# Rotary attention: how a chunk's row maxima are turned and laid into the query rows

## The chip, the cores and the metric

One Trainium2 chip; the kernel runs on one of its cores. The metric is device time in microseconds (us) of one execution, the median of several runs. Engines are named as the profile names them: PE is TensorE (PEld its weight loads), DVE is VectorE, ACT is ScalarE, POOL is GpSimd, and SP is SyncE, which does nothing here but issue DMAs. Each engine works through its own queue in order and waits on semaphores for the others.

## The reference

The program is a chain of four two-part layers on an input of shape (4, 1024, 128). The change touches one part, the rotary attention of the second layer, with H = 16 heads of 8 channels:

```python
def _L1_attn_ref(x, w_qkv, w_out, b_out):
    qkv = x @ w_qkv
    q, k, v = jnp.split(qkv, 3, axis=-1)
    ...
    q = q * cos + rotate_half(q) * sin
    k = k * cos + rotate_half(k) * sin
    dots = jnp.einsum('bhid,bhjd->bhij', q, k) * scale
    attn = jax.nn.softmax(dots, axis=-1)
    out = jnp.einsum('bhij,bhjd->bhid', attn, v)
    ...
    return out @ w_out + b_out
...
x = x + _L1_attn_ref(_layernorm(x, axis=-1), ...)
```

Each query row's softmax needs the greatest score of that row first, so that the exponentials do not overflow.

## The kernel before

**Tiles.** A batch has 1024 queries and 16 heads. The attention takes four heads at a time: 4 batches x 4 groups of heads = 16 tasks, each with its rows in a ring of three sets of tiles. Of a head g, tile `qz` holds 64 partitions: rows 0 to 31 are the rotated queries, split into a rounded and a remaining part, with one column for each query; rows 32 and 33 are for the row maximum, rounded part and remainder; the other rows are zero. `kz` holds the keys in the same way with 1.0 in rows 32 to 63. A product of `kz` and `qz` over those 64 rows therefore gives the score minus the maximum (the stored maxima are negated), once rows 32 and 33 are filled.

**Two passes.** A task is cut into 2 chunks of 512 queries, a chunk into 8 units. There are 16 x 2 = 32 chunks and 256 units, and the main loop takes one unit in each step k. The *first pass* (`greatest`, L1165) multiplies 128 queries by 512 keys for two heads into a PSUM tile `two` of 128x1024, and one DVE instruction reduces it to the negated maxima of each row (`nm`, L1173). The *second pass* (`scores`, L1194, then `values`) runs 11 units later (`LEAD`): it multiplies 128 keys by the chunk's 512 queries into a PSUM tile `s`, ACT takes the exponential (`e`, L1201), and PE multiplies that by the values into `o`. A step has two halves, and each half issues on PE, in this order: an `s` product, two `two` products, an `s` product, eight `o` products. The first half takes heads 2 and 3 in the second pass, the second half heads 0 and 1.

**Between the passes: `shifted` (L1175).** It runs once for each chunk. At the end of the chunk's last first-pass step (k = 8c+7) DVE takes the smaller of the two halves' values (`least`, L1178), rounds it into one element of `top` (L1179) and puts the remainder beside it (L1180). `top` is a zeroed tile of 128 x 4 (128 queries each) x 4 heads x 32. One step later (k = 8c+8) PE transposes its four 128x128 pieces into a PSUM tile `tp` (L1184), which takes one of the two buffers of `two`. ACT copies the 128x512 result to `sh` (L1188), in which head g has its two rows at partitions 32g and 32g+1, and SP issues one DMA for each head (L1191), 2 rows of 512 floats, into rows 32 and 33 of `qz`. The second pass of the chunk starts at step k = 8c+11.

**Order of the work.** On PE the order is the program's own (a manual schedule of PE alone). On DVE, ACT, POOL and SP a planner orders the instructions by its estimates. `tile`s with several buffers are waited for by buffer. DMAs on SP take eight semaphores in turn. On SP's queue the other work of this stage is `l1_spread` (L1124): eight DMAs a task that bring the next task's queries and keys, with a POOL instruction that zeroes rows 32 and 33 (L1132). `l1_rings` (L1056) allocates the rings and has POOL fill them, among them two `top` tiles (L1068).

Of the kernel before, what the change touches and what calls it, by code (L numbers as in the profile page):

```python
# [11 lines left out]
F32 = mybir.dt.float32  # L12
F32R = mybir.dt.float32r
# [3 lines left out]
ALU = mybir.AluOpType  # L17
AX = mybir.AxisListType

P = 128  # L20
B, S, D = 4, 1024, 128
# [3 lines left out]
HALF = 512  # L25
# [7 lines left out]
RING = 3  # L33
# [516 lines left out]
class Macaron:  # L550
# [505 lines left out]
    def l1_rings(self, pool):  # L1056

        fill = self.nc.gpsimd
        for tag, n, shape, dtype in (
            ("qz", 2 * RING, [P, S], F32R), ("kz", 2 * RING, [P, S], F32R), ("top", 2, [P, 4, 4, 32], F32),
        ):
            self.ring[tag] = [self.t(pool, shape, f"{tag}{i}", dtype) for i in range(n)]
        for z in self.ring["top"]:
            fill.memset(z, 0.0)  # L1068
        for tag, value in (("qz", 0.0), ("kz", 1.0)):
            for z in self.ring[tag]:  # L1070
                for j in range(2):
                    fill.memset(z[64 * j + 32 : 64 * j + 64, :].bitcast(F32), value)
# [61 lines left out]
    def l1_attn(self, m, c1, f):  # L1134

        nc = self.nc
        scale = HD ** -0.5
        LEAD = 11
        v = nc.vector
        PE = mybir.EngineType.PE  # L1140
        with ExitStack() as ctx:
# [5 lines left out]
            wp = enter(self.sb("l1a"))  # L1147
# [4 lines left out]
            two = lambda shape=(P, S): self.t(p1, list(shape), "two")  # L1152
            qz, kz, tops = (self.ring[tag] for tag in ("qz", "kz", "top"))
            of = lambda z, n, g: z[2 * (n % RING) + g // 2][64 * (g % 2) : 64 * (g % 2) + 64, :]
# [10 lines left out]
            def greatest(unit, pair, nm):  # L1165
                n, (c, it, h) = unit // 16, (unit // 8, unit % 8 // 2, unit % 2)
                at = (c % 2 * 4 + it) * P
                s = two((P, 2, HALF))
                for j in (1, 0):
                    g = 2 * pair + j  # L1170
                    self.mm(s[:, j, :], of(qz, n, g)[:, at : at + P], of(kz, n, g)[:, h * HALF : (h + 1) * HALF])
                    yield
                v.tensor_reduce(nm[:, it, h, 2 * pair : 2 * pair + 2], s, AX.X, ALU.max, negate=True)  # L1173

            def shifted(chunk, nm):  # L1175
                top, n = tops[chunk % 2], chunk // 2
                least = self.t(wp, [P, 4, 4], "least")
                v.tensor_tensor(least, nm[:, :, 0, :], nm[:, :, 1, :], ALU.min)  # L1178
                v.tensor_copy(top[:, :, :, 0].bitcast(F32R), least)  # L1179
                v.tensor_tensor(top[:, :, :, 1], least, top[:, :, :, 0], ALU.subtract)  # L1180
                yield
                tp = two((P, HALF))
                for i in range(4):
                    nc.tensor.transpose(  # L1184
                        tp[:, i * P : (i + 1) * P], top[:, i].rearrange("p g r -> p (g r)"), self.c0["ident"]
                    )
                sh = self.t(wp, [P, HALF], "sh", F32R)
                nc.scalar.copy(sh, tp)  # L1188
                for g in range(4):
                    z = of(qz, n, g)[32:34, chunk % 2 * HALF : (chunk % 2 + 1) * HALF]  # L1190
                    nc.sync.dma_start(out=z.bitcast(F32), in_=sh[32 * g : 32 * g + 2, :].bitcast(F32))  # L1191
                yield

            def scores(unit, pair, es):  # L1194
# [137 lines left out]
            for k in range(units + LEAD + 1):  # L1332
                at = k
                first = k if k < units else None
                second = k - LEAD if 0 <= k - LEAD < units else None
                if k % 16 == 2 and RING <= k // 16 + 1 < 4 * B:
                    self.l1_spread(k // 16 + 1)
                    values_of(k // 16 + 1)
                if k == 1:
                    running.append(chain(*late))  # L1340
                if first is not None and first % 8 == 0:
                    nms[first // 8] = self.t(wp, [P, 4, 2, 4], "nm", bufs=3)
                es = {}
                for pair in range(2):
                    top = greatest(first, pair, nms[first // 8]) if first is not None else iter(())
                    part = scores(second, 1 - pair, es) if second is not None else iter(())
                    for one in (part, top, top, part, top):
                        next(one, None)
                    if pending:
                        unit, then = pending  # L1350
                        if unit % 8 == 0 and pair == 0:
                            o = self.t(pa, [P, HALF], "o")
                        values(unit, o, then, pair)
                if pending and unit % 8 == 7:
                    running.append(normalized(unit // 8, o))
                pending = (second, es) if second is not None else None
                if first is not None and first % 8 == 7:
                    running.append(shifted(first // 8, nms[first // 8]))
                running = [r for r in running if next(r, self) is not self]
# [543 lines left out]
```

## Time and profile before

| what | us |
|---|---|
| median of three runs | 2524.29 |
| lowest, highest | 2516.03, 2534.74 |
| the profiled execution | 2518.22 |
| its span | 2516.5 |
| the rotary attention in it | about 731 to 1545 |

| engine | busy in the span | share |
|---|---|---|
| PE | 2205.0 | 88% |
| DVE | 1746.7 | 69% |
| ACT | 1557.2 | 62% |
| POOL | 1073.8 | 43% |

The profile is one execution. A row of a group of instructions gives the line of the kernel, the engine, the operation, the tile written and the tiles read, the shapes and the count; then the busy time and the mean ns of one; then the idle time of that engine just ahead of them and what ended it. The timeline lists instructions by start, with equal neighbours merged: start, length, engine, line. Ends of matmuls are modelled and overlap, so the wall time of PE is read from starts. "issue" is idle time that no shown wait explains. Semaphores that DMAs raise are in the trace's records with their times.

### The profile page before, as it was taken

What the parts mean: (1) busy time and instruction counts of PE and PEld (TensorE: products, weight loads), DVE (VectorE), ACT (ScalarE), POOL (GpSimd) and SP (SyncE); (2) the same over time, 40 slices, a digit from 0 to 9 for tenths busy, and PEclk for the clock granted to TensorE, in tenths of its full rate; (3) what the DMA queues carried; (4) which work ended last, traced back from release to release, by engine and by line L of the source; (5) the groups of instructions that cost most, each with busy time, mean ns of one, the idle gap of its engine ahead of it and who ended that gap; (6) DMA issues with size and microseconds to landing.
All of it is one profiled execution on the core that took longest, in us unless ns stands there. A gap on an engine that the chain in (4) does not pass through costs nothing. (4 is left out here: it accounts for less than half of the span.)

```text
span 2516.5 us, 44437 instructions
## 1 busy us (share of the span) xinstructions
PE 2205.0 (88%) x15631; PEld 1402.3 (56%) x15631; DVE 1746.7 (69%) x2883; ACT 1557.2 (62%) x3917; POOL 1073.8 (43%) x1124
## 2 busy tenths in 40 slices
PE   4888784987979999999999999988998978688996
PEld 4877773767654334334333334577886978433332
DVE  2497999971448888888998992552656552398995
ACT  3766673844537777788787786554554554556564
POOL 3778874668352201220220000067554557254553
PEclk8999997988988999999999999999998989899998
DMA  6866763557651200210120000178665679100000
GB/s 229 289 202 228 245 203 128 166 159 228 188 178 56 56 19 18 65 56 18 52 83 20 25 2 11 32 251 286 214 204 194 211 256 300 57 1 5 9 5 17
DMA packets 135694, 312.40 MB, mean 124 GB/s; under 512 B 20752, under 2 KB 70032, under 8 KB 135344
## 3 DMA queue, kind: packets, MB, share of 16 engines
q1 hardware_dynamic: 110320, 253.28, 30.9%
q0 software_dynamic: 25152, 56.28, 7.9%
q8 instruction: 125, 2.05, 0.3%
q14 instruction: 97, 0.79, 0.1%
HBM read 259.86 MB, written 49.09 MB: 123 GB/s over the span
## 5 line engine op out<-in xcount | busy, mean ns | idle before, releaser
L1173 DVE TENSOR_REDUCE nm<-two 128x2 f32<-128x1024 f32 x512 | 623.1, 1223 | 72.0 <-PE s L593 43.7
L1201 ACT ACTIVATE e<-s 128x512 f32<-128x512 f32 x1024 | 558.4, 598 | 133.5 <-PE s L593 120.3
L296 POOL DMA_INDIRECT e_xg<-rows,g_source x333 | 359.0, 1078 | 483.9 <-DVE g_target L296 232.4
L296 ACT ACTIVATE e_h<-bank,e_w 128x128 f32<-128x128 f32 x1332 | 381.8, 378 | 252.6 <-PE bank L296 133.4
L870 POOL DMA_INDIRECT res<-e_y,g_target x333 | 380.4, 1142 | 177.7 <-issue 40.5
L296 PE MATMUL bank<-e_x,e_w 128*128 128x128 f32 x2664 | 385.1, 286 | 28.7 <-DMA e_w<-in_l0m_dram 17.8
L296 PE MATMUL bank<-e_w,e_h 128*128 128x128 f32 x2664 | 389.3, 283 | 10.9 <-ACT e_h L296 10.2
L593 PE MATMUL s<-qz,kz 64*128 64x512 f32 x1024 | 383.9, 450 | 2.9 <-ACT e L1201 2.8
L296 PEld LDWEIGHTS bank<-e_x,e_w 128*128 128x128 f32 x2664 | 350.1, 201 | 46.6 <-issue 22.6
L593 PE MATMUL two<-kz,qz 64*128 64x512 f32 x1024 | 359.3, 458 | 8.6 <-DVE nm L1173 8.0
L296 PEld LDWEIGHTS bank<-e_w,e_h 128*128 128x128 f32 x2664 | 352.3, 198 | 21.3 <-ACT e_h L296 15.5
L593 PE MATMUL o<-e,va 128*32 128x256 f32 x4096 | 329.2, 392 | 7.4 <-ACT os L1218 6.9
L593 PEld LDWEIGHTS s<-qz,kz 64*128 64x128 f32 x1024 | 157.5, 186 | 206.0 <-issue 97.4
L296 DVE TENSOR_TENSOR e_y<-bank,e_w 128x128 f32<-128x128 f32 x202 | 57.6, 286 | 212.9 <-PE bank L296 202.8
L593 PEld LDWEIGHTS o<-e,va 128*32 128x32 f32 x4096 | 81.6, 108 | 192.5 <-issue 174.2
L296 PE MATMUL bank<-c,e_xg 128*128 128x128 f32 x333 | 95.4, 291 | 102.9 <-DMA e_xg<-rows,g_source 72.1
L1132 POOL MEMSET qz<- 2x1024 f32 x52 | 49.1, 945 | 309.1 <-PE s L593 306.9
L296 ACT ACT_TABLE_LOAD x130 | 166.8, 1283 | 9.3 <-PE bank L296 7.0
L593 PEld LDWEIGHTS two<-kz,qz 64*128 64x128 f32 x1024 | 142.7, 188 | 26.7 <-DVE nm L1173 23.1
L296 ACT COPY e_x<-bank 128x128 f32<-128x128 f32 x181 | 49.7, 276 | 116.3 <-PE bank L296 112.6
L296 PEld LDWEIGHTS bank<-c,e_xg 128*128 128x128 f32 x333 | 48.9, 148 | 117.9 <-DMA e_xg<-rows,g_source 53.1
L1111 POOL TENSOR_TENSOR h<-h 128x512 f32<-128x512 f32 x12 | 15.4, 1281 | 227.0 <-DVE h L1107 172.5
(316 smaller groups left out, 3440.0 us busy)
## 6 DMA issues: line engine op xcount, KB each, us to landing
e_w<-in_l0m_dram SPq DMA_DIRECT2D x177, 578.0 KB
e_w<-in_l2m_dram SPq DMA_DIRECT2D x156, 578.0 KB
c_y<-res SPq DMA_DIRECT2D x30, 512.0 KB
stack<-s POOLq DMA_DIRECT2D x48, 256.0 KB
rows<-g_xt SPq DMA_DIRECT2D x16, 512.0 KB
qz<-stack SPq DMA_DIRECT2D x64, 128.0 KB
kz<-stack SPq DMA_DIRECT2D x64, 128.0 KB
e_xg<-rows,g_source POOLq DMA_INDIRECT x333
```

What stands on the lines that cost most here:

```text
L296: return call(*a, **k)
L593: self.nc.tensor.matmul(out, lhsT, rhs, start=start, stop=stop)
L870: ins = real.gpsimd.indirect_dma_start(out=res[:, :], out_offset=at(target[:, k : k + 1]), in_=y, in_offset=None)
L1111: nc.gpsimd.tensor_tensor(whole, turned[:, 0, :], turned[:, 1, :], ALU.add)
L1132: self.nc.gpsimd.memset(z[at + 32 : at + 34, :].bitcast(F32), 0.0)
L1173: v.tensor_reduce(nm[:, it, h, 2 * pair : 2 * pair + 2], s, AX.X, ALU.max, negate=True)
L1201: nc.scalar.activation(e, o, AF.Exp, scale=scale)
```

## The change

The two parts of the maxima of four heads and four blocks of queries are 32 columns. They are now kept side by side in a `top` of 128 x 4 heads x 2 parts x 4 blocks, without zeros between them. One transpose turns them into 32 rows of 128, ACT copies those to `sh` (now 32x128), and eight DMAs, one for each head and part, each take 4 rows of 128 floats and write them side by side as one row of 512 floats of `qz`. The two fills of `top` are gone. The three DVE instructions stay, with the block index innermost.

```diff
-            ("qz", 2 * RING, [P, S], F32R), ("kz", 2 * RING, [P, S], F32R), ("top", 2, [P, 4, 4, 32], F32),
+            ("qz", 2 * RING, [P, S], F32R), ("kz", 2 * RING, [P, S], F32R), ("top", 2, [P, 4, 2, 4], F32),
         ):
             self.ring[tag] = [self.t(pool, shape, f"{tag}{i}", dtype) for i in range(n)]
-        for z in self.ring["top"]:
-            fill.memset(z, 0.0)
...
                 least = self.t(wp, [P, 4, 4], "least")
-                v.tensor_tensor(least, nm[:, :, 0, :], nm[:, :, 1, :], ALU.min)
-                v.tensor_copy(top[:, :, :, 0].bitcast(F32R), least)
-                v.tensor_tensor(top[:, :, :, 1], least, top[:, :, :, 0], ALU.subtract)
+                halves = [nm[:, :, h, :].rearrange("p i g -> p g i") for h in range(2)]
+                v.tensor_tensor(least, *halves, ALU.min)
+                v.tensor_copy(top[:, :, 0, :].bitcast(F32R), least)
+                v.tensor_tensor(top[:, :, 1, :], least, top[:, :, 0, :], ALU.subtract)
                 yield
-                tp = two((P, HALF))
-                for i in range(4):
-                    nc.tensor.transpose(
-                        tp[:, i * P : (i + 1) * P], top[:, i].rearrange("p g r -> p (g r)"), self.c0["ident"]
-                    )
-                sh = self.t(wp, [P, HALF], "sh", F32R)
+                tp = two((32, P))
+                nc.tensor.transpose(tp, top.rearrange("p g r i -> p (g r i)"), self.c0["ident"])
+                sh = self.t(wp, [32, P], "sh", F32R)
                 nc.scalar.copy(sh, tp)
                 for g in range(4):
-                    z = of(qz, n, g)[32:34, chunk % 2 * HALF : (chunk % 2 + 1) * HALF]
-                    nc.sync.dma_start(out=z.bitcast(F32), in_=sh[32 * g : 32 * g + 2, :].bitcast(F32))
+                    for r in range(2):
+                        z = of(qz, n, g)[32 + r : 33 + r, chunk % 2 * HALF : (chunk % 2 + 1) * HALF]
+                        rows = sh[8 * g + 4 * r : 8 * g + 4 * r + 4, :]
+                        nc.sync.dma_start(out=z.rearrange("r (i q) -> r i q", i=4).bitcast(F32), in_=rows.bitcast(F32))
                 yield
```

## The prediction

> **What bounds the kernel now.** The page first: all that the change touches lies in the rotary attention, so I asked for the busy times of that stage and of one of its last chunks, where nothing else runs.
>
> ```profile
> core 0: us, PE busy (x) PEld busy (x) DVE busy (x) ACT busy (x) POOL busy (x), PEclk, DMA share, GB/s
> 731.00:1545.00 814.00, 790.02 (x6694) 319.47 (x6690) 690.86 (x769) 619.86 (x1146) 122.22 (x159) 0.98 0.13 37
> 1493.00:1515.00 22.00, 21.64 (x200) 8.53 (x198) 20.22 (x23) 18.31 (x35) 0.00 (x0) 1.00 0.01 2
> ```
>
> PE is busy 97% of the stage, DVE 85%, ACT 76%, at a granted clock of 0.98. PE's own order repeats every 1.23 us (the starts of `s` below: 1497.59, 1498.82, 1500.05), and the reduction of L1173 takes 1.223 us, so a late PE is not made up for, and neither is a late DVE.
>
> Then the groups of the touched lines and of the reduction in that stage:
>
> ```profile
> L1173 DVE TENSOR_REDUCE nm<-two 128x2 f32<-128x1024 f32 x512 | 623.1, 1223 | 72.0 <-PE s L593 43.7 <-PE two L593 24.4
> L1184 PE MATMUL two<-c,top 128*128 128x128 f32 x128 | 20.6, 285 | 4.1 <-DVE top L1180 3.6
> L1188 ACT CAST sh<-two 128x512 fp32r<-128x512 f32 x32 | 18.8, 586 | 27.3 <-PE two L1184 27.2
> ```
>
> The transposes and the copy are some 39 us of busy time, but of two engines and with overlaps. How much is on the path, the timeline of chunk 30 shows:
>
> ```profile
> 1493.76 0.19 DVE L1180 TENSOR_TENSOR top<-least,top 128x16 f32<-128x16 f32 x1
> 1493.86 1.22 DVE L1173 TENSOR_REDUCE nm<-two 128x2 f32<-128x1024 f32 x1
> ...
> 1494.10 0.63 PE L1184 MATMUL two<-c,top 128*128 128x128 f32 x4
> ...
> 1494.76 0.59 ACT L1188 CAST sh<-two 128x512 fp32r<-128x512 f32 x1 [0.32 <-PE two L1184]
> 1495.13 0.19 PEld L593 LDWEIGHTS two<-kz,qz 64*128 64x128 f32 x2 [0.30 <-DVE nm L1173]
> ...
> 1495.41 2.49 SPq L1191 DMA_DIRECT2D qz<-sh  x4
> ...
> 1500.05 0.49 PE L593 MATMUL s<-qz,kz 64*128 64x512 f32 x1
> ...
> 1500.39 0.39 PE L593 MATMUL s<-qz,kz 64*128 64x512 f32 x1
> ```
>
> Three things are to be seen. `tp` holds one of the two buffers of `two`, so the next `two` product waits for the reduction that runs beside the transposes (1493.86 + 1.22 = 1495.08; PE goes on at 1495.13): PE idles 0.30 us whatever the transposes take. The four issues hold SP for 2.49 us. And the chunk's second pass starts at 1500.05 with head 2, head 3 follows at 1500.39: these need the third and fourth DMA. By the trace's semaphore records a DMA of L1191 has landed 1.67 us (median of 128) after its issue began; the fourth began at 1497.33 and landed at 1499.0, so head 3 has 1.4 us to spare.
>
> Last the rows of single DMAs, for a price of the new ones:
>
> ```profile
> L1191 SPq DMA_DIRECT2D qz<-sh x128: 562/563/732, 756.9 to 1518.9; - x128
> L1130 SPq DMA_DIRECT2D qz<-stack x64: 302/371/1716, 626.0 to 1410.5; - x64
> L296 SPq DMA_DIRECT2D stack<-s x16: 518/539/750, 524.1 to 618.5; - x16
> L296 SPq DMA_DIRECT2D out_dram<-x x8: 332/332/350, 2295.1 to 2509.2; - x8
> ```
>
> (min/median/max ns that one issue holds SP.)
>
> **The change part by part.**
>
> *Three transposes fewer.* Four take 0.63 us from the first start, one alone 0.301: 0.11 us each, 0.33 a chunk. By the starts in the trace, in 17 of the 32 chunks PE then waits for the reduction as above (it resumes 0.05 us after it): nothing is gained. In the other 15 PE comes late to the transposes, with work of other parts in front of it, and 0.26 to 1.6 us pass after the reduction: there 0.33 is gained. Sum: 15 x 0.33 = 5.0 us. Bounds: 0, and 32 x 0.33 = 10.6. The new transpose has 32 weight columns where the old had 128; no row shows an f32 transpose of 32 columns, but a plain f32 product of 128 columns (`e_x`, `e_w`) has a median of 275 ns beside 273 for L1184, so it stays at one such step. [...]
>
> *A smaller copy.* 512 columns take 0.586; ACT copies of 128x128 from PSUM (`e_x<-bank`) have a median of 0.266. I take 0.28: 0.31 less a chunk. ACT is 76% busy, and after the copy PE waits for the reduction, not for `tp`'s buffer, which the copy frees at 1495.35 and the next but one `two` product needs at 1496.36. So it only brings the DMAs forward. The DVE instructions keep their 16 elements (175, 177, 189 ns). The two fills of `top` (0.52 us each on POOL, at 537 and 547, before this stage) have no waiter that the trace shows: 0, at most 1 us.
>
> *Four DMAs more a chunk, on SP's queue.* The starts of L1191's issues lie 0.641 us apart (mean; 0.563 and the semaphore step between). The new DMA is of the same kind, from `sh` to `qz` on the same queue, four pieces of 512 B in place of two of 2 KB; its price no row shows. From below: the cheapest issue on SP, 0.302, so 0.38 apart. From above: a DMA from SBUF whose pieces differ on both sides (`stack<-s`, 0.539) takes 0.207 more than one whose rows agree (`out_dram<-x`, 0.332); put on top of 0.563 that is 0.77, so 0.85 apart. I take 0.641, its nearest row, and the same 1.67 to land. The last issue then begins 7 x 0.641 = 4.49 after the first instead of 3 x 0.641 = 1.92: 2.56 later, less 0.33 and 0.31 from the two parts above: the last row lands 1.92 us later against the transposes. SP has idle time for it: behind the eight in its queue are only `l1_spread`'s loads, needed more than ten steps later.
>
> [...]
>
> *What is late next.* `s` of head 3 waits for DMAs seven and eight; queued behind it on PE are the eight `o` products and the next `two`, so DVE and ACT run dry with it and the stall is paid in full. Head 3's margin over its landing, from the trace: in ten of the 17 chunks 1.36 to 1.50, mean 1.43, so 0.49 each, 4.9; chunk 7 has 1.12: 0.8; the other six have 2.16 or more: nothing. In the 15 late chunks PE arrives 0.33 earlier, so the shift is 2.25: margins of 1.60, 2.08, 0.90, 0.93, 1.18, 1.23 and 0.29 (the last chunk, with no first pass beside it) give 0.65 + 0.17 + 1.35 + 1.32 + 1.07 + 1.02 + 1.96 = 7.5; the rest have over 2.25. Stalls 13.2, gain 5.0: **+8.2 us**.
>
> **Where the sum stands.** On the profiled execution 2518.2 + 8 = 2526. That execution is 6 us under the median of the runs, so I give 2524.3 + 8 = 2533 with rounding. A change of under 1%, 25 us, is about what a measurement of this kernel can't tell from none.
>
> **The rivals.**
>
> *Dearer issues (slower).* At 0.85 apart the shift is 7 x 0.85 - 1.92 - 0.64 = 3.4, and nearly every chunk stalls: the ten by 1.9 (19), chunk 7 by 2.3, the seven late ones together 18, twelve more by 0.4 to 1.2, together 11; 51 less 5 is +46: 2570. It passes +25 us from 0.745 apart, an issue of 0.67. For it: the new DMA does reshape, 4 rows into one, and has 512 B pieces. Against it: both sides can be walked as four equal pieces, as the old one's as two. Beyond it lies a later landing, which acts the same way: each 0.1 us costs 2 to 3 us.
>
> *Cheap issues.* At 0.38 apart the shift is 0.1, only the last chunk stalls (0.1), and the gain of 5 stays: 2519. For it: 64 loads of L1130 are issued at 0.302 to 0.371. Against it: they come from DRAM and have 32 rows.
>
> *All of the removed work counts (faster).* 96 x 0.11 of PE and 32 x 0.31 of ACT on the path: 10.6 + 9.9 = 20 us, 2504. Against it: the 0.30 us that PE waits for the reduction, and ACT's idle share.
>
> **How the numbers follow.** Forecast 0.46, dearer issues or landings 0.38, cheap issues 0.10, all counted 0.06. The forecast and the cheap case are within 1% but for the spread of the runs, and most of the dear case is beyond. All counted is under 1%, and only with that spread over it, so faster 0.05. I put slower at 0.41 and same at 0.54. The range: below, the cheap case less the 8 us by which the lowest run lies under the median, 2511; above, the dear case and 0.1 us more to land or the run spread, some 10 us, 2580. The forecast's own range, from 0.60 to 0.745 apart (+4 to +25) and the same spread of 8, is 2520 to 2557.
>
> **What would show it.** Right: L1191's successor (now eight a chunk) 0.6 to 0.66 apart; the copy at 0.27 to 0.3; in the last chunks PE idle of some 0.5 us just ahead of `s`, ended by a DMA into `qz`, and the stage longer by 5 to 15 us. Wrong: issues at 0.67 or more, with waits of 1 to 2 us there; no waits there at all; or a different order on DVE or ACT, which the planner sets and no row of before can tell.

## The result, and the profile after

| | before | after |
|---|---|---|
| median, us | 2521.2 (20 runs) | 2537.18 (20 runs) |
| lowest, highest | 2508.74, 2534.74 | 2529.4, 2544.88 |
| the profiled execution | 2518.22 | 2544.88 |
| its span | 2516.5 | 2543.1 |
| the attention stage in it | 809.8 | 830.9 |

The ratio is 1.0063, 95% interval 1.0049 to 1.0076: 16 us slower. The *stage* is counted here and below from the start of the first `two` product to the start of the last `s` product; it is what the runs are compared by, since the rest of the program is not touched. It grew by 21.1 us in the profile. A second profile of the changed kernel (the last experiment) has 831.4, so that growth is no chance of one execution. The first profile is of the slowest of its 20 runs and takes 10.8 us longer behind the stage too; the second profile does not (976.3 us behind the stage, 976.1 before the change). In both the stage begins earlier than before the change, by 5.3 and 2.2 us; why was not pursued.

The touched groups of the changed kernel, from the profile's groups by line (line numbers shift by 2 to 4: the reduction is now L1171, the transpose L1182, the copy L1184, the DMAs L1189):

```profile
L1171 DVE TENSOR_REDUCE nm<-two 128x2 f32<-128x1024 f32 x512 | 623.4, 1223 | 89.9 <-PE s L593 64.7 <-PE two L593 21.1
L593 PE MATMUL s<-qz,kz 64*128 64x512 f32 x1024 | 389.8, 454 | 20.9 <-DMA qz<-sh 11.6 <-ACT e L1199 9.2
L593 PEld LDWEIGHTS two<-kz,qz 64*128 64x128 f32 x1024 | 143.3, 190 | 25.9 <-DVE nm L1171 18.3 <-ACT sh L1184 5.3 <-issue 0.9
L1182 PE MATMUL two<-c,top 128*32 128x128 f32 x32 | 8.9, 278 | 4.3 <-DVE top L1179 3.9
L1184 ACT CAST sh<-two 32x128 fp32r<-32x128 f32 x32 | 8.1, 254 | 16.9 <-PE two L1182 16.9
```

The transposes went from 20.6 to 8.9 us of busy time, the copy from 18.8 to 8.1; one transpose takes what one took (278 ns, was 285). Two idle times are new: `s` waits for a DMA into `qz` (11.6 us, nothing before), and the weight loads of `two` wait for the copy (5.3, before 0.5). DVE, which sets the pace together with PE, is idle 89.9 us ahead of its reductions instead of 72.0.

The new DMAs on SP (min/median/max ns that an issue holds SP):

```profile
L1189 SPq DMA_DIRECT2D qz<-sh x256: 572/573/747, 750.5 to 1533.1; - x128
```

Their starts are 0.636 us apart in the mean (median 0.618), and the median landing is 1.61 us after the issue began. Both prices are nearly those of the old DMA (0.641 and 1.67). The timeline of chunk 30, to set beside the one of before:

```profile
1505.52 1.22 DVE L1171 TENSOR_REDUCE nm<-two 128x2 f32<-128x1024 f32 x1
...
1505.75 0.27 PE L1182 MATMUL two<-c,top 128*32 128x128 f32 x1
...
1506.06 0.26 ACT L1184 CAST sh<-two 32x128 fp32r<-32x128 f32 x1
1506.37 0.19 PEld L593 LDWEIGHTS two<-kz,qz 64*128 64x128 f32 x2 [0.23 <-ACT sh L1184]
...
1506.38 5.00 SPq L1189 DMA_DIRECT2D qz<-sh  x8
...
1511.32 0.46 PE L593 MATMUL s<-qz,kz 64*128 64x512 f32 x1
...
1512.55 0.47 PE L593 MATMUL s<-qz,kz 64*128 64x512 f32 x1 [0.53 <-ACT e L1199]
```

Two things are to be read from it. First, the next `two` product starts 0.62 us behind the transpose, not 1.04 as before: it no longer waits for the reduction (which ends at 1506.74) but for the copy. Second, head 3's `s` starts at 1512.55, 1.23 us after head 2's instead of 0.34. The timeline names ACT for that wait, but the exponential that it means was long done; the eighth DMA, issued at 1510.80, landed at 1512.42, and `s` follows 0.13 us later. In 21 of the 32 chunks head 3's `s` starts 0.09 to 0.14 us behind that landing. From the transpose to head 3 it is 6.80 us instead of 6.29, half a microsecond lost. From chunk 19 to chunk 31 the loss is 0.48 a chunk in the mean.

Three chunks lose far more. Chunk 10, from the same profile's timeline:

```profile
1022.54 5.00 SPq L1189 DMA_DIRECT2D qz<-sh  x8
...
1026.14 2.09 POOL L1114 DMA_DIRECT2D stack<-s  x4
...
1027.52 0.47 PE L593 MATMUL s<-qz,kz 64*128 64x512 f32 x1 [0.40 <-ACT e L1199]
...
1030.59 0.46 PE L593 MATMUL s<-qz,kz 64*128 64x512 f32 x1 [2.37 <-DMA qz<-sh]
...
1031.85 0.79 PE L593 MATMUL s<-qz,kz 64*128 64x512 f32 x1
```

POOL's four stores of the next batch's preparation (256 KB each) start at 1026.14. The seventh and eighth DMA, issued at 1026.35 and 1026.97, land 2.63 and 3.49 us later instead of 1.61. PE waits 2.37 us, and the products behind that wait run at half speed (0.79 for 0.49). The rows of the stretches before and behind the wait (the share of the DMA engines is the last but one column, the granted clock the one before it):

```profile
1027.00:1030.50 3.50, 0.81 (x7) 0.29 (x3) 2.03 (x2) 1.09 (x3) 3.35 (x6) 1.00 0.83 227
1031.20:1034.60 3.40, 3.40 (x22) 1.29 (x15) 1.23 (x1) 2.03 (x4) 1.31 (x3) 0.50 0.98 299
```

Chunks 2 and 18 look the same. Together the three add 12.6 of the stage's 21.1 us (3.7, 4.4 and 4.5). In the same chunks before the change all four landed 1.66 to 1.68 us after their issue; the last of them was issued 1.0 us ahead of the stores.

### The profile page after: what moved, and what is told of

Same layout as the page of the kernel before. It is cut to its first block, busy times and chain, and to the rows that moved or that the text cites. A ratio compares the mean times of both kernels' runs of the same rounds, so it can differ in the third digit from the quotient of the medians.

```text
span 2543.1 us, 44449 instructions
## 1 busy us (share of the span) xinstructions
PE 2224.2 (87%) x15535; PEld 1405.5 (55%) x15535; DVE 1746.4 (69%) x2883; ACT 1552.5 (61%) x3917; POOL 1071.3 (42%) x1122
## 5 line engine op out<-in xcount | busy, mean ns | idle before, releaser
L1171 DVE TENSOR_REDUCE nm<-two 128x2 f32<-128x1024 f32 x512 | 623.4, 1223 | 89.9 <-PE s L593 64.7
L593 PE MATMUL s<-qz,kz 64*128 64x512 f32 x1024 | 389.8, 454 | 20.9 <-DMA qz<-sh 11.6
```

The lines of the kernel that those rows point to most:

```text
L593: self.nc.tensor.matmul(out, lhsT, rhs, start=start, stop=stop)
```

## The experiments

In the expectations, theory A is: only a landing that comes after PE's turn costs time. Its rivals C to G are given with each. Four questions are asked in turn: are the landings the cost; what do the stores add; does an issue cost anything by itself; where does the gain come from.

**Four DMAs with the new packing.** Each head's two rows, eight rows of `sh`, are laid by one DMA:

```diff
-                    for r in range(2):
-                        z = of(qz, n, g)[32 + r : 33 + r, chunk % 2 * HALF : (chunk % 2 + 1) * HALF]
-                        rows = sh[8 * g + 4 * r : 8 * g + 4 * r + 4, :]
-                        nc.sync.dma_start(out=z.rearrange("r (i q) -> r i q", i=4).bitcast(F32), in_=rows.bitcast(F32))
+                    z = of(qz, n, g)[32:34, chunk % 2 * HALF : (chunk % 2 + 1) * HALF]
+                    rows = sh[8 * g : 8 * g + 8, :]
+                    nc.sync.dma_start(out=z.rearrange("r (i q) -> r i q", i=4).bitcast(F32), in_=rows.bitcast(F32))
```

> The changed kernel, but each head's two rows are laid by one DMA of 8 rows of 128 (four DMAs a chunk, as in the kernel before; the one packed transpose and the small copy stay). Theory A (the time is lost because the last of eight issues lands after PE wants head 3): the last issue begins 4 x 0.636 = 2.5 us earlier, no wait of PE on a DMA into qz is left, and the 0.33 to 0.42 us a chunk that the smaller transpose saves stays: 5 to 13 us faster than before, ratio 0.995 to 0.998. Theory B (the packing itself costs: the planner's order, the slots of two, the small copy): still 10 to 20 us slower than before, ratio 1.004 to 1.008.

2511.46 against 2524.44 in the same session: 0.9956 (0.9932 to 0.998), faster than the kernel before. No wait of `s` for a row's DMA is left (eight DMAs: 11.6 us). The stage is 798.3 us, 32.6 less than with eight DMAs and 11.5 less than before the change. So the packing alone gains, and the eight DMAs lose nearly three times as much.

**Eight DMAs with the old packing.** The kernel before, each of a head's two rows laid by its own DMA:

```diff
-                    z = of(qz, n, g)[32:34, chunk % 2 * HALF : (chunk % 2 + 1) * HALF]
-                    nc.sync.dma_start(out=z.bitcast(F32), in_=sh[32 * g : 32 * g + 2, :].bitcast(F32))
+                    for r in range(2):
+                        z = of(qz, n, g)[32 + r : 33 + r, chunk % 2 * HALF : (chunk % 2 + 1) * HALF]
+                        nc.sync.dma_start(out=z.bitcast(F32), in_=sh[32 * g + r : 32 * g + r + 1, :].bitcast(F32))
```

> The kernel before, with its four transposes and its copy of 512, but each head's two rows are laid by two DMAs of one row of 512 (eight a chunk). Theory A: the last landing moves by 4 x 0.636 = 2.5 us against margins of mostly 1.4, with nothing saved: stalls sum to 22 us by the margins, and to some 33 with three collisions like those of the changed kernel: ratio 1.008 to 1.013. Theory B: eight DMAs cost nothing by themselves, ratio 0.998 to 1.002.

2582.62 against 2524.44, 1.0241 (1.0207 to 1.0276): the direction was right, the size over twice what was expected. The waits, from the list of PE's waits (total, times, longest):

```profile
PE s L593 <- DMA qz<-sh: 29.2, 30, 3.0
```

A clean chunk lasts 23.20 us instead of 21.97, 1.23 more, close to what the shift of the last landing gives (2.56 less the margin of 1.43 is 1.13). The rest is in chunks where landings were late: 2, 10 and 18, beside the stores, grew by 6.4, 8.5 and 8.3 us with half clock behind the waits; and there were late landings in other chunks (see the last section).

**Another order.** The changed kernel with the DMAs of heads 2 and 3, which PE needs first, ahead of those of 0 and 1:

```diff
-                for g in range(4):
+                for g in (2, 3, 0, 1):
```

> The changed kernel, eight DMAs, but the heads are laid in the order 2, 3, 0, 1, the order in which the second pass takes them. Theory A: heads 2 and 3 have landed 2.5 us earlier, heads 0 and 1 are wanted 1.23 us later than 2 and 3, so no wait is left but some 1 to 2 us in each of the chunks where the stores of the preparation delay the last landings: 2 to 12 us faster than before, ratio 0.995 to 0.999. Theory C (what matters is that SP is held for 5 us a chunk and the loads behind it come late): as slow as the changed kernel, ratio 1.004 to 1.008.

2513.98 against 2524.44, 0.9958 (0.9935 to 0.998). The same eight issues, in another order, take 23.6 us off the stage (807.3). The rival that SP's time itself is what costs falls. Four waits are left, for heads 0 and 1, mainly in the chunks with stores (total, times, longest):

```profile
PE s L593 <- DMA qz<-sh: 4.9, 4, 1.9
```

**The stores earlier.** The changed kernel with the next batch's preparation two steps sooner, meant to bring the stores ahead of the DMAs:

```diff
-            coming = [(64 * b - 61, self.l1_prepare(p2, "s", prep, m, c1, b)) for b in range(1, B)]
+            coming = [(64 * b - 63, self.l1_prepare(p2, "s", prep, m, c1, b)) for b in range(1, B)]
```

> The changed kernel, with the preparation of the next batch begun two steps earlier (63 in place of 61), so that POOL's four stores of a prepared half start some 5 us before, and not beside, the seventh and eighth DMA in chunks 2, 10 and 18. Theory A with collisions (three long stalls of 2.4 us, each followed by 3.4 us of half the clock, make some 12 us of the loss): 8 to 14 us faster than the changed kernel, ratio to before 1.000 to 1.004, and no stretch of half clock after those chunks. Without collisions as a cause: ratio 1.005 to 1.008, as the changed kernel.

A miss: 2556.89 against 2524.44, 1.0131 (1.0103 to 1.0159), slower than the changed kernel itself. PE's waits for the rows doubled:

```profile
PE s L593 <- DMA qz<-sh: 22.8, 18, 2.8
```

The preparation has several groups of four stores, and the shift was chosen by the one beside chunks 2, 10 and 18. Two steps sooner, stores begin 2.8 us behind the first issue in chunks 4, 9 and 17, 3.1 behind it in chunk 1 and 3.6 in chunks 12 and 20; there the last DMAs land 3.4 to 4.6 us after their issues. In chunks 2, 10 and 18, where the stores now come ahead, it is the first DMAs that land late (3.6 to 3.9), and nobody waits for these. The mechanism holds, the remedy was wrong.

**The stores later.** Instead one step later, `64 * b - 60`, with the eight DMAs still in the order of the heads:

> The changed kernel with its eight DMAs in the order of the heads; only the next batch's preparation, whose four stores on GpSimd fell beside the seventh and eighth DMA of chunks 2, 10 and 18, starts one step later (64b - 60 in place of 64b - 61). Theory A with the stores as the second mechanism: the stores are issued about 2.5 us later, behind the last landing, so that all eight land 1.6 us after their issue in those chunks too; the three waits of 2.4 us shrink to about 0.5 and the half clock behind them goes; the 12.6 us of these three chunks shrink to about 2, so 0.999 to 1.003 of the kernel before, the waits of s for a row's DMA 5 to 9 us in all, none above 1.3. Theory E (the three jumps are due to something else in those steps of the preparation, as the order on DVE or POOL): the jumps stay wherever the stores go, 1.005 or more.

This one, and those below that are set against 2638.92 or 2648.05, ran on two other chips. These are slower ahead of the stage (which begins at 772 to 782 us there, at 725 to 731 in the other runs), so ratios and stages are compared. 2648.97 against 2638.92, 1.003 (1.0011 to 1.0049), stage 819.8: 11.1 us less than the changed kernel. The waits:

```profile
PE s L593 <- DMA qz<-sh: 4.5, 9, 0.9
```

All eight land within 1.65 us in chunks 2, 10 and 18, and no stretch of half clock is left there. That the jumps were due to something else in those steps falls.

**Order and later stores together, still eight DMAs.**

> The changed kernel with all its eight DMAs a chunk, and both things that made them late taken away: heads in the order 2, 3, 0, 1, and the next batch's preparation one step later (64b - 60). Theory A (eight issues cost nothing where none lands after PE's turn): no wait of s for a row's DMA above 1 us in all, the attention stage 798 to 800 us as with four DMAs (798.3 and 798.0), the ratio as the best so far, 0.991 to 0.997. Theory C (eight issues or their traffic cost by themselves): the stage stays above 803, the ratio at 0.998 or more.

2512.11 against 2521.49, 0.996 (0.9942 to 0.9978), stage 798.9, one wait of 0.5 us for a row. This is the same stage as with four DMAs (798.3), so eight issues a chunk cost nothing where none lands after its turn.

**Four DMAs and the new order.**

> Both remedies together: one transpose, one DMA for each head's two rows (four a chunk), heads in the order 2, 3, 0, 1. Theory A (only a landing that comes after PE's turn costs time): neither remedy had waits worth more than 5 us left, so there is nothing more to take; 0.993 to 0.998 of the kernel before, no wait of s for a DMA of a row above 1 us in all, as with four DMAs alone. Theory D (issues and landings cost something also where nobody waits, by SP's queue or by DMA traffic): the two gains add up, under 0.992.

2620.8 against 2638.92, 0.9931 (0.9903 to 0.9959), stage 798.0. The ratio alone doesn't separate the theories well; the stage does: 0.3 us less than with four DMAs alone. The two remedies do not add up.

**The second experiment in the new order**: the old packing, eight DMAs of one row, heads 2, 3, 0, 1.

> The kernel before with four transposes and the copy of 512 columns, eight DMAs of one row each as in the second experiment (1.024), but heads in the order 2, 3, 0, 1. Theory A: the eight issues cost nothing by themselves; heads 2 and 3 land 3 x 0.62 + 1.6 us after the first issue as in the kernel before, heads 0 and 1 are needed 1.23 us later than head 2; 0.998 to 1.004, the waits of s for a row's DMA under 6 us, what is left of them beside the stores in chunks 2, 10 and 18. Theory C (SP's issues or the traffic of eight DMAs cost whatever is waited for): 1.012 or more.

2665.98 against 2638.92, 1.0091 (1.0063 to 1.0119): between the two theories. The clean chunks speak plainly: chunk 29 takes 21.96 us (21.97 before the change), with eight DMAs in it. Of the stage's 25.4 us over the kernel before 19.7 come from chunks 2, 10 and 18 (6.2, 7.1 and 6.4), where the eighth DMA landed 5.0 to 5.5 us after its issue. What I had left out is how much later a one-row DMA lands beside the stores.

**The transposes put back.** From here on the question is the gain. The four-DMA kernel in the new order, with the transpose done four times, into four parts of `tp`, the last of which is copied (0.26 us, as with one):

```diff
-                tp = two((32, P))
-                nc.tensor.transpose(tp, top.rearrange("p g r i -> p (g r i)"), self.c0["ident"])
+                tp = two((32, HALF))
+                for i in range(4):
+                    nc.tensor.transpose(
+                        tp[:, i * P : (i + 1) * P], top.rearrange("p g r i -> p (g r i)"), self.c0["ident"]
+                    )
...
-                nc.scalar.copy(sh, tp)
+                nc.scalar.copy(sh, tp[:, 3 * P :])
```

> The best version so far (one transpose, four DMAs, heads 2, 3, 0, 1) with the transpose done four times, into four parts of tp, of which the last is copied: PE's removed work is put back, the shorter copy stays. Its attention stage was 798.0 us in the profile, against 809.8 before the change: a gain of 11.8. Theory F (in the clean chunks the next product into two takes the buffer that tp leaves, so it waits for the copy behind the transposes; all of the transposes' 0.33 us then counts in all 32 chunks): the stage takes 10.6 us longer than with one transpose, about 808.5, and the ratio is 0.997 to 1.001. Theory G (as predicted: PE waits for the reduction beside the transposes in 17 of the chunks, so only the late 15 lose): 5 us longer, 803, 0.994 to 0.998, with PE starting the next product at the same distance from the first transpose as with one.

2648.69 against 2648.05, 0.9999 (0.9974 to 1.0024), stage 808.5: theory F's sum to the tenth. That it fits so well is partly luck: F has 0.33 us in every chunk, but clean chunk 29 takes 0.45 longer (21.98 against 21.53 with one transpose), and the others 0.01 to 0.75, but for one that got shorter. What the weight loads of `two` wait for:

```profile
L593 PEld LDWEIGHTS two<-kz,qz 64*128 64x128 f32 x1024 | 142.8, 189 | 27.2 <-DVE nm L1171 23.2 <-ACT sh L1187 1.2 <-issue 1.0
```

With four transposes the wait is for the reduction again (23.2 us, for the copy 1.2), and the next product starts 1.04 us behind the first transpose in the clean chunks, as in the kernel before. With one it is 0.61. Chunk 30 shows that this is not the buffer that comes free first:

```profile
1544.46 1.22 DVE L1171 TENSOR_REDUCE nm<-two 128x2 f32<-128x1024 f32 x1
...
1545.33 0.26 ACT L1187 CAST sh<-two 32x128 fp32r<-32x128 f32 x1 [0.28 <-PE two L1183]
...
1545.73 0.19 PEld L593 LDWEIGHTS two<-kz,qz 64*128 64x128 f32 x2 [0.33 <-DVE nm L1171]
```

The copy is done at 1545.59, the reduction at 1545.68, and the product waits for the reduction all the same.

**A second copy.** The same kernel with one transpose and another copy of `tp` behind the first, into a tile that is not read:

```diff
+                nc.scalar.copy(self.t(wp, [32, P], "sh2", F32R), tp)
```

> The best version so far with a second copy of tp behind the first, into a tile that nobody reads: ACT works 0.26 us longer a chunk and tp's buffer comes free that much later, while the DMAs start as early. Theory F: where the next product into two waits for the copy it waits until the reduction's buffer or the second copy, whichever the buffers' order gives: if tp's buffer is still taken, up to 0.3 us more in each of some 17 to 25 chunks, 5 to 8 us in the stage, 803 to 806, 0.994 to 0.998; if the other buffer is taken, the reduction ends the wait as before, about 1.04 us behind the first transpose, the same 5 to 8 us. Theory G (the copy never ends a wait of PE): no change to 798, 0.992 to 0.995.

2638.84, 0.9962 (0.9943 to 0.9981), stage 801.7: 3.7 us more than with one copy, a little below what theory F gave, and not nothing.

```profile
L593 PEld LDWEIGHTS two<-kz,qz 64*128 64x128 f32 x1024 | 143.3, 189 | 29.5 <-DVE nm L1171 18.4 <-ACT sh L1185 8.9 <-issue 0.9
```

The wait for the copy grew from 5.1 to 8.9. The two copies overlap (the second starts 0.16 us after the first), so the buffer comes free 0.16 later, and the next product starts at 0.77 instead of 0.61, in 22 of 31 chunks. The copy ends that wait.

**The changed kernel once more.**

> The changed kernel itself once more, beside the last one, for a second profile. By the readings so far its attention stage is some 32 us longer than with four DMAs: 828 to 833, with stalls at the landings in the clean chunks, three longer ones in chunks 2, 10 and 18 and the half clock behind these; ratio 1.004 to 1.009. If the three long stalls were chance of one profiled execution, they are in other chunks or missing here, and the stage is 818 to 822.

2538.61 against 2521.49, 1.007 (1.0043 to 1.0097); stage 831.4, the long waits again in chunks 2, 10 and 18 with 3.4 us of half clock behind each. Two smaller parts differ: this profile has a wait of 1.6 us with half clock in chunk 26, the first one has 6.8 us of half clock at the stage's end.

The stages, put together, split the change's +21.1 into three parts. The last two are worth one edit each; the first is what is left of the change when nobody waits for a landing:

| part | from the stages | us |
|---|---|---|
| the packing: one transpose, the short copy | eight DMAs that nobody waits for, 798.9, less before, 809.8 | -10.9 |
| head 3's two DMAs last in the order | stores later, 819.8, less the same in the new order, 798.9 | +20.9 |
| the stores beside them in three chunks | the changed kernel, 830.9, less stores later, 819.8 | +11.1 |

The four-DMA kernel, which differs from the one before in the packing alone, gives -11.5 for the first part. The line between the last two is less sharp: taken chunk by chunk, 7.7 of the 11.1 lie in chunks 2, 10 and 18 and 2.2 at the stage's end, where the run with later stores has no half clock; the rest is spread over other chunks.

## Why the prediction was right, and where not

The time came out as forecast, 2537 for 2533, slower by less than 1%. The growth did not: 8 us were forecast and 16 measured, and the stage grew by 21.1 where the prediction's own sign of being right was 5 to 15. That the time is off by only 4 us is partly luck: the gain was put too low by 5.9 us and the stalls by 18.8, which partly cancel, and the median before is 3 us lower over twenty runs than over the three that the forecast started from. Of its steps:

*The price of the eight DMAs* held. 0.641 us apart was predicted, 0.636 measured; 1.67 to land, measured 1.61. With it the rivals of dear and of cheap issues fall as prices.

*What is late next* held: head 3's `s` waits for the eighth DMA and is paid in full. In a clean chunk 0.49 was predicted and 0.48 measured.

*"In 17 of the 32 chunks ... nothing is gained"* is the step that failed. I took the wait for the reduction as fixed, because the row of before showed it. But `two` has two buffers, and the next product waits for whatever used its own one last: the reduction, or the copy of `tp`. In the trace its weight load waits on one semaphore. Before the change that is DVE's in 29 of 31 chunks; in the changed kernel it is ACT's in 22, and the copy, done 0.56 us behind the transpose, lets the product start ahead of the reduction's end (0.99). So the changed program has another order of buffers, which the prediction had named as a sign of being wrong (an order that the planner sets). The transposes put back made it DVE's in 24 chunks again, though in the clean chunks the copy was done first, and cost 10.5 us; the second copy cost 3.7. The packing was worth 10.9 us, not 5.0; and the copy, which I had called off the path, ends the wait. That the order follows the times that the planner estimates is likely, but no run tested it.

*The stalls* were put at 13.2 us; they cost 32.0 (20.9 and 11.1). Part of that is the same error: what a clean chunk gains ahead of the landing, 0.42 us, it waits for again at the landing, so gain and stall both grew and the net of 0.48 stayed. The other part was not in the sum at all: the two last DMAs, moved 2.5 us later in SP's queue, came beside POOL's four stores in three chunks, landed 1.0 and 1.9 us late, and PE's long wait was followed by a stretch of half clock (3.4 us at 0.50). The text did say that a later landing acts as a dearer issue does; it did not look for what else is under way at the new time, though the times of those stores were in the trace.

*That all of the removed work counts* was given 20 us. About half of it did (10.9), but only a kernel that doesn't stall at the landings shows it.

## What to carry to other kernels

When a step is moved to later, look up in the trace what else is on the DMA engines at its new time, and order transfers by who needs them first: here the order of four numbers in a loop was worth 24 us of the stage. When a tile has two buffers, the row of before shows only the wait that this program's order of buffers gives; a change of the work beside it can give another order, and then work that had no wait in any row counts. So look up in the new trace what each product waits for. The version that beats both kernels keeps the one transpose and lays a head's two rows with one DMA (0.9956); eight DMAs in the order of need, clear of the stores, do as well (0.996).

## What the hardware showed

A small transfer landed late beside large ones of another queue. SP's seventh and eighth 2 KB DMA in chunks 2, 10 and 18, under way beside POOL's four 256 KB stores (the DMA engines were 83% busy, by the row of chunk 10 above), landed in 2.6 to 3.5 us instead of 1.61. With the stores one step later all eight landed within 1.65 us in those chunks; with the stores two steps sooner the last DMAs of six other chunks landed 3.4 to 4.6 us after their issues.

The same 2 KB, cut into more packets, landed later there. Eight DMAs of a quiet chunk are 64 packets in the changed kernel (half of them 512 B of data, the others the 4 B of semaphores) and 256 with one row each (128 B). SP's queue around chunk 30 of the changed kernel (packets, MB, share of 16 engines):

```profile
q1 hardware_dynamic: 64, 0.02, 0.7%
```

and around chunk 29 of the second experiment:

```profile
q1 hardware_dynamic: 256, 0.02, 1.9%
```

Beside the stores the eighth DMA of the one-row form landed 4.9 to 5.5 us after issue, that of the changed kernel 3.2 to 3.5. It was late elsewhere too: 40 of its 256 DMAs took over 2.0 us to land in the second experiment, 12 of the changed kernel's. Nine of the 40 were beside the stores; the other 31 each had a packet of 8 or 16 KB of the queue that the trace calls "instruction" under way between issue and landing, and so had 15 of the 216 that landed in time. Whether these packets are the cause was not tried, and no run shows why the finer cut landed later.

PE's granted clock fell to 0.5 for 3.4 us behind the waits of 1.9 to 2.5 us in chunks 2, 10 and 18 of the changed kernel's two profiles; in the run with later stores, whose longest wait for a row is 0.9 us, it did so nowhere from chunk 2 to the transposes of chunk 27.

When a wait fell mattered here as well as how long it was. In each of the 13 traces the stretches of half clock begin whole multiples of 3.413 us apart. Cut on that grid, from chunk 2 to the last `s`, the traces have 37 windows at full clock that half clock follows, with PE busy in 20 to 63% of each; of the 2731 other windows at full clock only 7 have PE busy less than 70%. The trace of before has one of the 37 (54% busy), the first profile of the changed kernel four (40, 30, 25 and 59%). One and the same wait of 1.6 us, ahead of the transposes of chunk 27, is followed by half clock in the second profile of the changed kernel and not in the first; in the first it lies across two windows, with PE busy 2.68 and 2.57 of their 3.41 us.
